# Pairwise bilinear products on one core: VectorE in the order of the text, and a later cut in two loads

## The chip, the cores and the metric

The kernel runs on one core of a Trainium2 chip. The metric is device time in microseconds (us) of one launch: the median of three runs, beside the time of one more execution that was taken with the hardware profiler. Differences below about 0.2% can't be told from no change here.

## The reference

For each of 4096 batch rows there are 32 fields of 64 numbers. Each field is multiplied by a 64x64 matrix W, and every pair of fields i < j (496 pairs) gives an elementwise product of the raw field i and the transformed field j, all in float32:

```python
vid = jnp.einsum('bfd,de->bfe', x, W)
idx_i, idx_j = jnp.triu_indices(F_, k=1)
return x[:, idx_i, :] * vid[:, idx_j, :]
```

The input has 33.6 MB and the output 520 MB, so nearly everything that the core does is to write products to HBM.

## The kernel before

**Tiles.** The batch is cut into 16 tiles of 256 rows. The host lays the data out so that the 128 partitions are two batch halves times 64 numbers, and a "unit" is 128 batch rows of one field (or of one pair): 128 float32, 512 bytes on each partition. A tile of input is 32 units; its output is 496 units.

**Memory.** One buffer, `mem`, of 445 units on each partition holds everything: the input tiles, at the units listed in `XPLACE`, and 70 store slots, listed in `SLOTS` as (number of units, first unit, seams). Slots lie on top of older slots and of input tiles that are no longer needed. The framework adds the waits that follow from overlap: a product that writes a unit waits until an earlier store that reads this unit has landed, and a load waits likewise. `vid`, the transformed fields of one tile, takes all of PSUM.

**Work of a tile.** TensorE makes `vid` from the input tile (line 172). VectorE then runs `tensor_tensor` multiplications (line 196), 345 of them over the 16 tiles. The generator `by_block` gives their order, and `products` cuts each block where a slot ends or where a slot has a seam. A product of m x w pairs has m*w*128 elements on each partition: a 5x16 product shows in the profile as 128x10240. When a product fills a slot up to its end, SP issues one DMA that stores the whole slot (line 199). The output order is the order in which the slots are filled, and a slot may hold the end of one tile and the beginning of the next.

**Loads.** Tile 0 comes first, then tiles 1 to 3 in one DMA, then tiles 5 and 4. Two later groups of five tiles each are loaded behind tile 4 and behind tile 9 (lines 205 to 207 start them, line 151 issues them). `CUTS` splits such a load of 160 fields into three DMAs. `load` returns these as `pieces`, and the next store after them gets a dependency on `pieces[-2]` (lines 200 to 202): SP does not issue it before the last load piece but one has landed. So the fields of the last piece are what may still be under way when SP issues that store. All DMAs, loads and stores, are issued by SP, in the order of the text, on one queue.

```python
CUTS = [[None, [(0, 51), (51, 64)]], [(0, 127), (127, 140), (140, 160)], [(33, 160), (20, 33), (0, 20)]]
...
                store = nc.sync.dma_start(out=out[:, begin:end, :], in_=ot)
                if pieces:
                    behind(store, pieces[-2])
                    pieces.clear()
```

**Order on the engines.** `tc.manual_schedule(engines={SP})` keeps SP's instructions in the order of the text. On the other engines the framework's scheduler orders the instructions; it may put an instruction ahead of an earlier one when it expects that one to wait.

**Slots at the places spoken of below.** Slot 60 is (112, 333): units 333 to 444. Slot 61 is (127, 158). Slot 62 is (127, 285): units 285 to 411. Slot 63 is (127, 64, 94): units 64 to 190. Slots 44, 45 and 46, around the last group of loads, are (120, 176), (116, 297) and (92, 160, 16).

Of the kernel before, what the change touches and what calls it, by code (L numbers as in the profile page):

```python
# [21 lines left out]
    [[6, 7, 8, 9, 10]],  # L22
    [[15, 14, 13, 12, 11]],
]
CUTS = [[None, [(0, 51), (51, 64)]], [(0, 127), (127, 140), (140, 160)], [(33, 160), (20, 33), (0, 20)]]
XPLACE = [317, 349, 381, 413, 32, 0, 285, 317, 349, 381, 413, 128, 96, 64, 32, 0]


# [24 lines left out]
def by_block():  # L53


    def within(lo):
        yield "step", lo, 2, 1, 0
        for k in range(2):
            yield "step", lo, 4, 2, k
        for i in (lo, lo + 8):  # L60
            yield "row", i + 4, i, 4, 4
        yield "row", lo + 8, lo, 8, 8

    yield from within(0)
    yield "row", 16, 0, 16, 16
    yield from within(16)


def products(blocks, at=0):

    for kind, a, b, c, d in blocks:
        if kind == "row":
            rows, n, i0, di, j0, dj = c, d, b, 0, a, 1
        else:
            rows, n, i0, di, j0, dj = 16 // b, c, a, b, a + c + d, b
        r = k = 0
        while r < rows:
            room = BREAKS[bisect_right(BREAKS, at)] - at
            if k or room < n:
                m, w = 1, min(n - k, room)  # L80
            else:
                m, w = min(rows - r, room // n), n
            yield at, m, w, i0 + r * di + k, di, j0 + r * dj, dj
            at += m * w
            if k + w == n:
                r, k = r + m, 0
            else:
                k += w
# [10 lines left out]
@with_exitstack  # L99
def pairwise_bilinear_kernel(  # L100
    ctx: ExitStack,
    tc: tile.TileContext,
    x0: bass.AP,
    x: bass.AP,
    out: bass.AP,
):

    nc = tc.nc
    NT = sum(len(tiles) for group in GROUPS for tiles in group)
    F = x0.shape[1] - 1 - PAD0
    D = P // 2
    NP = F * (F - 1) // 2

    BANK = 512 // C


    ctx.enter_context(tc.manual_schedule(engines={mybir.EngineType.SP}))

    const = ctx.enter_context(tc.tile_pool(name="const", bufs=1))
    psum = ctx.enter_context(
        tc.tile_pool(name="ps", bufs=1, space=bass.MemoryType.PSUM)
    )
    vid = psum.tile([P, F, C], F32)

    mem = const.tile([P, UNITS, C], F32)


    w2 = const.tile([P, D], F32)


    place = XPLACE[0]
    nc.sync.dma_start(  # L136
        out=mem.rearrange("p u c -> p (u c)")[:, place * C - D : (place + F // 2) * C],
        in_=x0.rearrange("p u c -> p (u c)")[:, C - D : (1 + F // 2) * C],
    )
    nc.sync.dma_start(out=mem[:, place + F // 2 : place + F, :], in_=x0[:, 1 + F // 2 : 1 + F, :])  # L140
    nc.vector.tensor_copy(w2, mem[:, place - 1, C - D :])  # L141
    loaded = 1

    def load(tiles, cuts=()):
        nonlocal loaded
        n = len(tiles) * F
        place = XPLACE[tiles[0]]
        at = (loaded - 1) * F
        loaded += len(tiles)
        return [  # L150
            nc.sync.dma_start(out=mem[:, place + lo : place + hi, :], in_=x[:, at + lo : at + hi, :])  # L151
            for lo, hi in cuts or [(0, n)]
        ]

    ready = mybir.DependencyInfo(mybir.DependencyClass.Sync, mybir.DependencyReason.DATA)

    def behind(later, earlier):
        tc.add_manual_dep(later.ins, earlier.ins.name, ready, reason="issued when that has landed")

    pieces = []  # L160
    groups, cuts = iter(GROUPS), iter(CUTS)
    for tiles, parts in zip(next(groups)[1:], next(cuts)):
        pieces = load(tiles, parts)

    for t in range(NT):
        xt = mem[:, XPLACE[t] : XPLACE[t] + F, :]


        for b in range(0, F, BANK):
            for h in range(2):  # L170
                half = slice(h * D, (h + 1) * D)
                nc.tensor.matmul(  # L172
                    vid[half, b : b + BANK, :],
                    lhsT=w2[half, :],
                    rhs=xt[half, b : b + BANK, :],
                    start=True,
                    stop=True,
                )

        for at, m, w, i, di, j, dj in products(by_block(), t * NP):  # L180
            slot = bisect_right(STARTS, at) - 1
            n = m * w
            begin, end = STARTS[slot], STARTS[slot + 1]
            ot = mem[:, SLOTS[slot][1] : SLOTS[slot][1] + SLOTS[slot][0], :]
            o = ot[:, at - begin : at - begin + n, :]
            if m == 1:
                left = xt[:, i : i + w, :]
                right = vid[:, j : j + 1, :].to_broadcast([P, w, C])
            else:
                o = o.rearrange("p (m w) c -> p m w c", m=m)  # L190
                right = vid[:, j : j + (m - 1) * dj + 1 : dj, :].unsqueeze(2).to_broadcast([P, m, w, C])
                if di == 0:
                    left = xt[:, i : i + w, :].unsqueeze(1).to_broadcast([P, m, w, C])
                else:
                    left = xt.rearrange("p (m d) c -> p m d c", d=di)[:, i // di : i // di + m, i % di : i % di + w, :]
            nc.vector.tensor_tensor(o, left, right, ALU.mult)  # L196
            at += n
            if at == end:
# [6 lines that stand above are left out]
        if t + 2 == loaded < NT:  # L205
            (tiles,) = next(groups)
            pieces = load(tiles, next(cuts))
# [45 lines left out]
```

## Time and profile before

| what | value |
|---|---|
| median of 3 runs (lowest, highest) | 1291.11 us (1290.9, 1291.38) |
| the profiled execution | 1290.48 us |
| its span, first to last instruction | 1288.7 us |
| TensorE clock granted, mean | 0.55 |
| HBM read, written | 33.59 MB, 520.09 MB |
| TensorE matmuls | 219.6 us in 512 instructions |
| VectorE idle until a store had landed | 168.1 us in 37 waits |

The profiled execution is 0.63 us below the median, and 1.8 us of it lie outside the span. "Landed" is the moment at which a DMA's semaphore is complete; the list of DMA issues gives the time from issue to landing. In the slices of the page each digit is a share in tenths, and 9 means 90% or more. When a window of a few microseconds is cut into slices, a packet (a piece of up to 65 KB, about 2.4 us on one DMA engine) counts in the slice in which it starts, so single slices there are spiky, and only a long run of zeros means idle engines. The trace also records every DMA packet with its start, duration and size; where the text gives times of single packets, they come from there. On each of the 16 DMA engines the last packet of a DMA is a write of 4 bytes, and from these one sees when each engine was through with that DMA.

### The profile page before, as it was taken

Reading aid. Unit: us, or ns where it says so; the run is one execution under the profiler, and the core shown is the slowest. Engines: PE = TensorE matmul, PEld = TensorE weight load, DVE = VectorE, ACT = ScalarE, POOL = GpSimd, SP = SyncE. Lnnn points to the kernel's source line nnn. Section 1 sums busy time; section 2 is a strip of 40 time slices with the busy share of each in tenths; the row PEclk is TensorE's granted clock in tenths of the full one; section 3 lists DMA queues with packets and bytes.
Section 4 is the critical chain, followed back from the end, with each engine's and each line's share of the span. In section 5 each row is a group of like instructions: output and inputs, shape, how many; then the busy total and the mean of one; then the engine's idle time right before and its main releaser. Section 6 shows DMA issues by size and latency. Waiting matters only on the chain.

```text
span 1288.7 us, 1651 instructions
## 1 busy us (share of the span) xinstructions
PE 219.6 (17%) x512; PEld 42.2 (3%) x512; DVE 1084.0 (84%) x346; POOL 0.2 (0%) x4
## 2 busy tenths in 40 slices
PE   4031221203120213040312111103031130312000
PEld 1000000000000000000000000000000000000000
DVE  6899988899967389899799992859999889999942
POOL 0000000000000000000000000000000000000000
PEclk8555555656555556565555655555555565555555
DMA  9999999999999999999999999999999999989999
GB/s 416 432 423 439 443 436 423 434 424 443 420 453 411 422 435 431 443 439 430 423 442 427 433 443 430 423 418 432 447 433 418 441 440 418 448 361 452 435 414 412
DMA packets 11672, 553.78 MB, mean 430 GB/s; under 512 B 1296, under 2 KB 1296, under 8 KB 1680
## 3 DMA queue, kind: packets, MB, share of 16 engines
q1 hardware_dynamic: 11664, 553.69, 99.6%
q8 instruction: 4, 0.07, 0.0%
q14 instruction: 4, 0.03, 0.0%
HBM read 33.59 MB, written 520.09 MB: 430 GB/s over the span
## 4 chain that ended last, share of the span: by engine, by line
DMA 50%; DVE 42%; issue 6%; DVEq 0%; SPq 0%
DMA out_dram<-mem 45%; DVE mem L196 42%; DMA mem<-in_r_x_dram 5%; DVEq L241 0%; SPq L151 0%; DVEq L196 0%; SPq L140 0%; SPq L136 0%; SPq L199 0%
## 5 line engine op out<-in xcount | busy, mean ns | idle before, releaser
L196 DVE TENSOR_TENSOR mem<-mem,vid 128x1024 f32<-128x1024 f32 (+16 forms) x345 | 1083.8, 3213 | 173.6 <-DMA out_dram<-mem 168.1
L172 PE MATMUL vid<-mem,w 64*64 64x512 f32 x512 | 219.6, 988 | 961.1 <-DVE mem L196 853.3
L172 PEld LDWEIGHTS vid<-mem,w 64*64 64x64 f32 x512 | 42.2, 198 | 1137.3 <-DVE mem L196 984.8
L141 DVE COPY w<-mem 128x64 f32<-128x64 f32 x1 | 0.2, 195 | 5.8 <-DMA mem<-in_r_x_dram 5.8
L221 POOL MEMSET const-bfloat16-1.0<- 128x1 bf16 x1 | 0.1, 102 | 0.0
L221 POOL MEMSET const-uint8-127<- 128x1 uint8 x1 | 0.1, 102 | 0.0
L221 POOL MEMSET const-float32-0.0<- 128x1 f32 x1 | 0.1, 98 | 0.2 <-issue 0.2
L221 POOL MEMSET const-float32-1.0<- 128x1 f32 x1 | 0.1, 98 | 0.0
## 6 DMA issues: line engine op xcount, KB each, us to landing
out_dram<-mem SPq DMA_DIRECT2D x15, 8128.0 KB, 28.3
out_dram<-mem SPq DMA_DIRECT2D x14, 7680.0 KB, 24.6
out_dram<-mem SPq DMA_DIRECT2D x6, 7168.0 KB, 26.2
out_dram<-mem SPq DMA_DIRECT2D x5, 7936.0 KB, 28.1
out_dram<-mem SPq DMA_DIRECT2D x3, 7424.0 KB, 22.6
out_dram<-mem SPq DMA_DIRECT2D x3, 5888.0 KB, 20.9
mem<-in_r_x_dram SPq DMA_DIRECT2D x2, 8128.0 KB, 38.7
out_dram<-mem SPq DMA_DIRECT2D x2, 8064.0 KB, 24.4
```

The lines of the kernel that those rows point to most:

```text
L141: nc.vector.tensor_copy(w2, mem[:, place - 1, C - D :])
L172: nc.tensor.matmul(vid[half, b : b + BANK, :], lhsT=w2[half, :], rhs=xt[half, b : b + BANK, :], start=True, stop=True,)
L196: nc.vector.tensor_tensor(o, left, right, ALU.mult)
L221: nc = _bacc.Bacc("TRN2", target_bir_lowering=False, num_devices=1, dynamic_dma_scratch_size=1024)
```

## The change

```diff
-CUTS = [[None, [(0, 51), (51, 64)]], [(0, 127), (127, 140), (140, 160)], [(33, 160), (20, 33), (0, 20)]]
+CUTS = [[None, [(0, 51), (51, 64)]], [(0, 127), (127, 134), (134, 160)], [(33, 160), (26, 33), (0, 26)]]
...
-    ctx.enter_context(tc.manual_schedule(engines={mybir.EngineType.SP}))
+    ctx.enter_context(tc.manual_schedule(engines={mybir.EngineType.SP, mybir.EngineType.DVE}))
```

The first edit moves the boundary between the second and the third piece of the two large loads: the second piece shrinks from 13 fields to 7, and the third grows from 20 to 26. The store behind each of the two loads, which waits for the second piece, is thus issued with 26 fields left under way in place of 20. The loads' total size and the number of DMAs stay. The second edit keeps VectorE's instructions, too, in the order of the text. TensorE's order remains the scheduler's.

## The prediction

> **What bounds the kernel now.** I read the page first, for the engine that is never free:
>
> ```profile
> span 1288.7 us, 1651 instructions
> ...
> PE 219.6 (17%) x512; PEld 42.2 (3%) x512; DVE 1084.0 (84%) x346; POOL 0.2 (0%) x4
> ...
> DMA  9999999999999999999999999999999999989999
> GB/s 416 432 423 439 443 436 423 434 424 443 420 453 411 422 435 431 443 439 430 423 442 427 433 443 430 423 418 432 447 433 418 441 440 418 448 361 452 435 414 412
> ...
> q1 hardware_dynamic: 11664, 553.69, 99.6%
> ```
>
> The 16 DMA engines are busy throughout; VectorE, at 84%, has room. One slice stands out: the 36th (1127.6 to 1159.8 us) has an 8 and 361 GB/s. So the time is bytes over DMA rate plus the time in which DMA engines have nothing to do, and such time lies in one place. I asked for the DMA view of 1125 to 1145 us, in slices of 0.5 us:
>
> ```profile
> DMA  9029980299502000000009000090000900009000
> GB/s 520 0 130 910 650 390 0 130 1300 390 260 0 130 0 0 0 0 0 0 0 0 2081 0 0 0 0 2081 0 0 0 0 2081 0 0 0 0 2081 0 0 0
> ```
>
> From 1131.5 to 1135.5 us no packet but one starts. By the packet records the engines end the store before at 1131.68 (first) to 1133.56 (last) and all start the next at about 1135.81; idle time, averaged over the 16, is 3.74 us. Elsewhere after the first load it sums to under 0.6 us. The chain of waits for 1090 to 1160 us says who was late:
>
> ```profile
> 1096.97 11.13 DVE mem L196 x6
> 1108.10 0.99 issue
> 1109.09 25.89 DVE mem L196 x8
> 1134.98 20.59 DMA out_dram<-mem
> ```
>
> VectorE works without a break until SP issues a store at 1134.98. The issues around it (DMA view of windows at 1089.3 and at 1106.7) show when the two stores before it land:
>
> ```profile
> out_dram<-mem SPq DMA_DIRECT2D x1, 7168.0 KB, 25.9
> ...
> out_dram<-mem SPq DMA_DIRECT2D x1, 8128.0 KB, 27.3
> ```
>
> The first is slot 60 (1089.29 + 25.9 = 1115.2), the second slot 61 (1106.74 + 27.3 = 1134.0). So slot 62 was issued 0.95 us after the queue's last store had landed. Why was VectorE late? The groups of 1111.0 to 1141.6 us, shapes apart:
>
> ```profile
> L196 DVE TENSOR_TENSOR mem<-mem,vid 128x10240 f32<-128x10240 f32 x1 | 10.8, 10809 | 0.0
> L196 DVE TENSOR_TENSOR mem<-mem,vid 128x7168 f32<-128x7168 f32 x1 | 7.6, 7611 | 0.0
> L196 DVE TENSOR_TENSOR mem<-mem,vid 128x2048 f32<-128x2048 f32 x3 | 6.8, 2276 | 0.0
> ...
> L196 DVE TENSOR_TENSOR mem<-mem,vid 128x768 f32<-128x768 f32 x1 | 0.9, 943 | 0.0
> ```
>
> Slot 62 wants, after its 33rd unit, two 4x4 products (2048 elements; the third in the group is another slot's), one 7x8 (7168) and one 1x6 (768). The 5x16 product (10240) belongs to slot 63 and stands after them in the text. In the trace it runs first, from 1111.36 to 1122.09, inside the last products of slot 62. I compared the shapes of all 345 products with the order that the generator gives: only here and at one place near 798 us does the trace differ from the text.
>
> **What the Trainium skill says.** "DMA: Bandwidth & Descriptors", section "Queues, rings and completion order": each DMA engine consumes its queue in ring order. The trace agrees; each engine starts a DMA right behind its own part of the one before. The section "Why a DMA increments its semaphore by 16 and not by 1" of that page: the engines finish independently and only the full count means landed. Here the 16 ends are 1.88 us apart before the gap and 0.16 us apart after it (1155.06 to 1155.22). The section "Specifications": the fabric's ceiling is 435 GB/s. In steady stretches stores land at 434 to 435 GB/s, so nothing is to be won from the rate.
>
> **Edit 1, VectorE in the order of the text, near 1111 us.** The scheduler had a reason: the first 4x4 product writes units 318 to 333, and unit 333 is read by slot 60's store, which lands at 1115.17. In the order of the text VectorE therefore idles from 1111.36 to 1115.22, 3.86 us. Then, by the starts in the trace (a product starts some 0.08 us before its forerunner's end): 2.20 + 2.20 + 7.53 + 0.94 = 12.87 us, and slot 62 is full at 1128.09. SP issues it at 1128.1, 6.9 us earlier. First packets come 0.83 us after an issue (1134.98 to 1135.81), so at 1128.95, before the first engine is free at 1131.68. The gap is gone.
>
> What it is worth: the end is set by the DMA engine that is last. It ended at 1133.56 and finished slot 62's store at 1155.22, after 21.66 us. Such a store (65024 bytes per partition) takes the last engine 19.17 us while the engines are apart (landings at 1061.22 and 1080.39): 2.49 us saved. The seven stores after it landed 19.24, 19.27, 18.76, 18.15, 19.24, 18.74 and 18.88 us apart with the engines in step; with the engines apart, as before the gap, stores of these sizes took 19.17, 19.17, 18.69, 18.10, 19.17, 18.69, and scaled 18.83: 132.28 - 131.82 = 0.46 us more. Sum 2.95 us. Bounds: 2.27 us, the last engine's own idle time (1133.56 to 1135.83), if it doesn't catch up; 3.74 us, the mean idle time of all 16, if it catches up fully. I take 2.95.
>
> What is late next: VectorE's idle 3.86 us reappears at slot 63, whose 5x16 product now comes last: full at 1145.4 instead of 1141.5. The store before lands at 1134.04 - 0.12 + 19.17 = 1153.1 (slot 61's landing trailed its last packet by 0.48 us, 0.12 more than others), 7.7 us later. Slot 64 is full at 1162.8 against a landing at 1172.3. VectorE's own waits of 1.46, 0.20, 1.41 and 1.53 us, all for landings that now come 2.5 to 2.9 us earlier, take up the delay; the last wait (15.03 us at 1250.32) moves with the landings. The smallest margin remains slot 69's 5.5 us. So the 3.86 us cost nothing.
>
> **Edit 1, near 798 us.** A 512-element product (0.68 us) of slot 46 ran ahead at 798.59, in VectorE's wait for a landing (to 809.40). In the text's order it follows at 835.3, in another such wait (17.64 us, to 852.99). Nothing.
>
> **Edit 2, the cut.** 6 fields are 393 KB, 0.9 us at 434 GB/s: SP issues the held stores at about 427.9 and 830.9 instead of 428.78 and 831.74. Before, the first engine was through with the loads at 429.60 and 832.58 and began the store at 429.62 and 832.61: at most 0.03 us is to be had, on engines that are not the last. Load packets cost bytes/27.03 plus 7 ns, with the count unchanged: nothing. The following stores on SP queue behind the held one, but they were ready within 2 us and had 17 us to spare. A loss can't be excluded by the trace of before: at the opposite turn, from store to load (402 and 805 us), the last store packets took 2384 in place of 2291 ns, and store plus load landed 1.24 us late. With loads then stores the last engine had its store's descriptors ready 1.8 us ahead and lost nothing (14.54 and 18.14 us, full rate). I take 0; the range holds 0 to 1.24 us at each of two places.
>
> Sum against the profiled execution: 1290.48 - 2.95 = 1287.5. Its time is 0.63 us under the median, so the median becomes 1291.11 - 2.95 = 1288.2.
>
> **Rivals.**
> - The turn costs: one or both held stores disturb the loads' tail by 1.24 us, 1289.4 to 1290.6. For: the opposite turn. Against: the last engine's case above. 10%.
> - No gain, 1291.1: the gap reopens elsewhere, or the scheduler's semaphores hold slot 62 back. It needs slot 62 to be full 5 us later than worked out. For: in-order VectorE can no longer pass over a late landing. Against: margins of 5 us or more at all other stores. 13%.
> - Slower: TensorE, which stays with the scheduler, is ordered anew around the fixed VectorE, and a group of matmuls that VectorE needs comes after those of the whole tile. A tile's matmuls are 219.6/16 = 13.7 us; a store has about 5 us of margin, so VectorE's wait counts from 5 us on, and one such tile costs 13.7 - 5 = 8.7 us net of its margin: 1297. Against: VectorE waited for TensorE once, 5.4 us, at the start. 10%.
> - More than worked out, 1287.0: a refill of instructions that now falls on another engine than the last one. 5%.
>
> **How the numbers follow.** 62% for 1288.2 (own range 1287.4 to 1288.9). What a measurement can tell from no change is 0.2%, 2.6 us: faster means below 1288.5. Of the main case about four fifths lie there: 0.62 x 0.8 + 0.04 = 0.54. Slower 0.10, the rest 0.36. The range of 1287.2 to 1291.2 takes in the first two rivals and leaves out the slow one and the tail.
>
> **What would show it.** Right: the 10240-element product after the 768 one; an idle VectorE of about 3.9 us before 1115.2; slot 62 issued near 1128; no empty slices at 1131 to 1136; slot 63 near 1145; the 16 ends of the last store 1 to 2 us apart; held stores issued 0.9 us earlier with no change in landings. Wrong: landings after 427 or 831 us that come later by a microsecond; a new store issued after the landing of the one before; VectorE waits on TensorE after the first tile.

## The result and the profile after

| | before | after |
|---|---|---|
| median of 8 runs (lowest, highest) | 1290.95 us (1290.4, 1291.38) | 1287.17 us (1286.98, 1287.57) |
| ratio, 95% interval | | 0.9971 (0.9962 to 0.9981) |
| the profiled execution, its span | 1290.48 us, 1288.7 us | 1287.35 us, 1285.6 us |

The change makes the kernel 3.8 us faster. That is 0.8 us more than forecast, and 1287.17 us lies 0.03 us below the low end of the stated range. The range was counted from a before of 1291.11 us; before measured 0.16 us less in this series.

The page of the kernel after, the lines that answer to those of before:

```profile
span 1285.6 us, 1654 instructions
...
PE 220.4 (17%) x512; PEld 42.4 (3%) x512; DVE 1083.6 (84%) x346; POOL 0.2 (0%) x4
...
DMA  9999999999999999999999999999999999999998
GB/s 414 419 440 440 436 420 447 420 442 418 443 432 431 428 433 420 438 438 429 445 423 447 434 419 439 419 426 435 438 433 422 441 439 423 443 427 427 434 443 385
...
q1 hardware_dynamic: 11664, 553.69, 99.8%
```

The 36th slice has a 9 and 427 GB/s now; only the last slice, in which the last store runs out, is below. The DMA view of 1125 to 1145 us, again in slices of 0.5 us:

```profile
DMA  5059565095659990699505985059555098256980
GB/s 260 0 260 1300 260 260 260 0 1300 260 260 260 390 910 520 0 260 780 780 260 0 260 1170 390 260 0 260 1300 260 260 260 0 1300 390 130 260 260 1170 390 0
```

The long run of zeros is gone: no two slices in a row are empty. VectorE, in the timeline of 1105 to 1150 us (start, length, what, and in brackets the idle time before it):

```profile
1114.69 41.39 DVE L196 TENSOR_TENSOR mem<-mem,vid 128x2048 f32<-128x2048 f32 x12 [2.61 <-DMA out_dram<-mem]
```

and in the groups of 1111 to 1117 us, shapes apart:

```profile
L196 DVE TENSOR_TENSOR mem<-mem,vid 128x2048 f32<-128x2048 f32 x2 | 4.5, 2282 | 2.6 <-DMA out_dram<-mem 2.6
```

So VectorE now waits 2.61 us for slot 60's landing, then runs slot 62's two 2048-element products; the 10240-element product is no longer ahead of them. SP issues slot 62 at 1127.60 us in place of 1134.98. Its issue line (DMA view at 1127.6 us) shows the landing, 1127.60 + 25.3 = 1152.9 us:

```profile
out_dram<-mem SPq DMA_DIRECT2D x1, 8128.0 KB, 25.3
```

The store ahead of it lands at 1133.74 us, so slot 62 is in the queue 6.1 us early.

### The profile page after: what moved, and what is told of

It reads as the page before. It is cut to its first block, busy times and chain, and to the rows that moved or that the text cites. A ratio compares the mean times of both kernels' runs of the same rounds, so it can differ in the third digit from the quotient of the medians.

```text
span 1285.6 us, 1654 instructions
## 1 busy us (share of the span) xinstructions
PE 220.4 (17%) x512; PEld 42.4 (3%) x512; DVE 1083.6 (84%) x346; POOL 0.2 (0%) x4
## 4 chain that ended last, share of the span: by engine, by line
DMA 46%; DVE 46%; issue 6%; DVEq 0%; SPq 0%
DVE mem L196 46%; DMA out_dram<-mem 41%; DMA mem<-in_r_x_dram 5%; DVEq L241 0%; SPq L151 0%; DVEq L196 0%; SPq L140 0%; SPq L136 0%; SPq L199 0%
## 5 line engine op out<-in xcount | busy, mean ns | idle before, releaser
L196 DVE TENSOR_TENSOR mem<-mem,vid 128x1024 f32<-128x1024 f32 (+17 forms) x345 | 1083.4, 3213 | 170.8 <-DMA out_dram<-mem 165.1
```

## The experiments

Each kernel is timed beside the kernel before on the same chip. The experiments are four series, each on another chip, and the median of before in them is 1291.03 to 1291.19 us, so a few tenths of a microsecond between kernels of different series are weak evidence. Traces are of one execution each. "Fields left" is the size of the last piece of a large load. All but the one with the cut alone have VectorE in the order of the text.

### Which edit, and which product

**Order alone.** The kernel before with the second edit only:

```diff
-    ctx.enter_context(tc.manual_schedule(engines={mybir.EngineType.SP}))
+    ctx.enter_context(tc.manual_schedule(engines={mybir.EngineType.SP, mybir.EngineType.DVE}))
```

> VectorE in the order of the text, the cut left at 140 and 20. Theory (the order fills the gap near 1131 us, the cut gives nothing): the whole gain, 1287.2 us, ratio 0.997; no empty slices at 1131 to 1136 us, slot 62 issued near 1127 us. If the cut costs about 0.6 us at the loads, as the shift of the landings after 427 and 831 us in the changed kernel suggests, this one is up to 0.6 us faster than the changed kernel: 1286.6 us. Rival (the cut is what helps): 1291 us.

Measured: 1288.12 us (1287.77 to 1288.56), ratio 0.9976 (0.9968 to 0.9985): 2.91 us faster than before. Slot 62 is issued at 1129.06 us. The DMA view of 1125 to 1145 us:

```profile
DMA  9920299202962029903098029920299202952029
GB/s 910 910 130 0 130 1431 390 130 0 130 1561 260 130 0 130 1561 390 0 130 0 1561 390 0 130 520 1300 130 0 130 1300 520 130 0 130 1561 260 130 0 130 1561
```

No gap. The order explains 2.9 of the 3.8 us. The suspicion that the cut costs something, read from one pair of traces, fell: without the cut the kernel is 0.95 us slower than the changed one, and the ranges of the runs don't touch.

**Cut alone.** The kernel before with the new `CUTS` line only.

> The cut at 134 and 26 alone, VectorE left to the scheduler. Theory: no gain, 1291.0 us, the gap near 1131 us stays; if the cut costs at the loads, landings after 427 and 831 us come 0.4 to 0.7 us later than before, and part of it vanishes in the gap, where all engines start together: at most 1291.5 us. Rival (the cut is what helps): 1287.2 us.

Measured: 1291.09 us (1290.8 to 1291.49), ratio 1.0002 (0.9993 to 1.001). The DMA view of 1125 to 1145 us:

```profile
DMA  5229552992623000000000090000900009000090
GB/s 260 130 130 1300 260 260 130 520 1040 130 260 130 130 0 0 0 0 0 0 0 0 0 0 2081 0 0 0 0 2081 0 0 0 0 2081 0 0 0 0 2081 0
```

The gap is there, and the cut gives nothing. So the cut is worth 0.95 us with the gap filled and nothing with it.

**One product back.** The changed kernel, with slot 63's 5x16 product put ahead of slot 62's last four and slot 63's first product, as the scheduler had it. The place near 798 us stays in the order of the text.

```diff
-        for at, m, w, i, di, j, dj in products(by_block(), t * NP):
+        listed = list(products(by_block(), t * NP))
+        if t == 14:
+            k = [p[0] for p in listed].index(7064)
+            listed.insert(k - 5, listed.pop(k))
+        for at, m, w, i, di, j, dj in listed:
```

> The changed kernel with one product moved: the 5x16 product of slot 63 stands ahead of the two 4x4 products of slot 62 again, as the scheduler had it; the other reordering, near 798 us, stays undone. Theory (this one product makes the gap): the whole gain is gone, 1291 us, slot 62 issued near 1135 us. Rival (the place near 798 us, or fixed order as such, gives the gain): 1287.2 us.

Measured: 1291.11 us (1290.89 to 1291.56), ratio 1.0001 (0.9992 to 1.0009). The chain of waits of this kernel for 1090 to 1165 us:

```profile
1108.61 0.99 issue
1109.60 25.89 DVE mem L200 x8
1135.49 20.59 DMA out_dram<-mem
1156.08 0.02 issue
```

The store is issued at 1135.49 us again, and the chain has the shape that it had before. One product out of 345 makes the gap, and the other reordering is worth nothing that shows.

### Why the cut is worth 0.95 us

**No hold.** The changed kernel without the hold behind the two large loads (the first one, behind tiles 5 and 4, stays):

```diff
                 if pieces:
-                    behind(store, pieces[-2])
+                    if t < 4:
+                        behind(store, pieces[-2])
                     pieces.clear()
```

> The changed kernel without the hold behind the two large loads: the two stores are issued as soon as their slots are full. Theory (the held stores' time of issue is covered by the loads in flight, so its size doesn't matter once descriptors are there in time): 1287.2 us within 0.5. Rival (a store that is ready behind a load disturbs the load's tail, more the earlier it is ready): 1288 to 1290 us, with the landings of the loads' pieces after 427 and 831 us later by half a microsecond or more.

Measured: 1288.26 us (1287.9 to 1288.51), ratio 0.9978 (0.997 to 0.9986): 1.1 us slower than the changed kernel, and the last pieces of the loads land 0.5 and 0.4 us later. The rival holds. SP's timeline of 815 to 833 us shows the second store issued 13 us earlier than in the changed kernel (831.51):

```profile
818.71 0.34 SPq L199 DMA_DIRECT2D out_dram<-mem  x1
```

In the packet records, packets of the last load piece (13312 bytes, about 0.50 us each) that took over 0.15 us more than most packets of this size, and the time that slow packets add, in the mean of the 16 engines:

```
                 first load     second load    time added, first and second load
changed kernel   3 of 128       0 of 128       0.03 us, under 0.01 us
without hold     31 of 128      31 of 128      0.74 us, 0.86 us
```

So stores that are ready far ahead do disturb the end of a load, and this is what the hold is good for. Single slow packets occur with the hold, too: a second trace of the changed kernel has three, one of them 1.15 us longer than the others.

**21, 28 and 32 fields left.** The changed kernel with other boundaries in both loads: (127, 139) and (21, 33), then (127, 132) and (28, 33), then (127, 128) and (32, 33). Theory B arose because TensorE, with the new cut, has one more instruction that only waits (12 in place of 11), and because its fourth refill of instructions moved from 1113 to 1102 us; the page counts the four refills in this line:

```profile
q8 instruction: 4, 0.07, 0.0%
```

> The changed kernel with 21 fields left in place of 26 (pieces end at 139, and begin at 21). A boundary inside a group of four fields gives TensorE one more wait, as with 26 and unlike with 20, and so its fourth refill of instructions falls near 1102 us as in the changed kernel, not near 1113. Theory A (the 0.95 us between 20 and 26 fields comes from the time of issue: with 20 the DMA engines that are through first wait for the held store): 1287.9 us, a little better than with 20, first store packets later than the first engine's end by up to half a microsecond. Theory B (it comes from the moved refill): 1287.2 us.

> The changed kernel with 28 fields left. The boundary falls between groups of four, so TensorE has as many waits as with 20, and the refill falls near 1113 us. Theory A (time of issue): 1287.2 us or a little less, no idle engines at the turn. Theory B (the moved refill): 1288.1 us.

> The changed kernel with 32 fields left, the store issued 0.9 us earlier still. If a store that is ready ahead of the loads' end disturbs their tail, as the slow load packets of the kernel without the hold suggest, it shows here first: some load packets of the last piece 0.2 to 0.8 us longer, and 1287.3 to 1288 us, between 26 fields and no hold (1288.26 us). If the disturbance needs a store that is ready long before: 1287.2 us.

Measured: 21 fields 1287.56 us (1287.34 to 1288.48), between the theories. 28 fields 1287.26 us (1286.93 to 1287.53), but TensorE has the one more instruction there, too, and the refill fell at 1101 us, so that run didn't tell the theories apart. 32 fields 1287.74 us (1287.21 to 1288.06): half a microsecond lost, as the first case of its expectation had it. Only one and three packets of the last pieces were slow, 0.07 us in the mean of an engine at each load, but that trace is of the fastest execution of this kernel; what the half microsecond went to is not shown. From 20 over 26 to 32 fields and to no hold, the time falls and rises again; 26 and 28 can't be told apart.

**The refill moved, the cut not.** Order alone, plus two matmuls of tile 0 issued twice (the last group of fields, both halves), which shifts TensorE's refills.

```diff
+            if t == 0 and b == F - BANK:
+                nc.tensor.matmul(vid[half, b : b + BANK, :], lhsT=w2[half, :], rhs=xt[half, b : b + BANK, :], start=True, stop=True)
```

> VectorE in the order of the text, the cut at 140 and 20 as before, and two of tile 0's matmuls issued twice (the last group of fields, both halves), so that TensorE's stream is some instructions longer and its fourth refill falls near 1100 us in place of 1114. Theory A (the 0.95 us between 20 and 26 fields is the time of issue): 1288.1 us, as with the order alone. Theory B (the moved refill): 1287.2 us.

Measured: 1287.81 us (1287.62 to 1288.55), with the refill at 1100.6 us: 0.31 us under the order alone, 0.6 above the changed kernel. So the moved refill alone doesn't bring the 0.95 us; whether it brings a third of them can't be told, since the two ranges overlap. The third refill moved as well, from 833.2 us with the order alone to 765.9.

**One load at a time.** The new cut in the second load only, then in the first only, and the changed kernel once more as the measure.

```diff
-[(0, 127), (127, 134), (134, 160)], [(33, 160), (26, 33), (0, 26)]
+[(0, 127), (127, 140), (140, 160)], [(33, 160), (26, 33), (0, 26)]    second load only
+[(0, 127), (127, 134), (134, 160)], [(33, 160), (20, 33), (0, 20)]    first load only
```

> VectorE in the order of the text, and the new cut at the second large load alone (26 fields left there, 20 at the first). The boundary inside a group of four fields, which gives TensorE its one more wait, is that of the first large load, so here the refill falls near 1114 us as before. Theory A (time of issue, mostly at the second load, where engines were seen idle with 20 fields left): 1287.4 us. Theory B (the moved refill): 1288.1 us.

> VectorE in the order of the text, and the new cut at the first large load alone (26 fields left there, 20 at the second); TensorE has its one more wait and the refill falls near 1101 us. Theory A: 1287.9 us. Theory B: 1287.2 us.

> The changed kernel itself, beside the two, as the measure for them: 1287.2 us.

Measured: second only 1287.48 us (1287.34 to 1287.75) with the refill at 1114.9 us; first only 1287.81 us (1287.47 to 1288.29) with the refill at 1100.5; changed kernel 1287.22 us (1287.0 to 1287.34). Theory A had 1287.4 and 1287.9, theory B 1288.1 and 1287.2. As the whole account B falls. First only and the changed kernel ran in one series, have the third and the fourth refill at the same places within a microsecond (832.4 and 1100.5, 832.2 and 1101.5 us), and differ in the cut at the second load alone: it gives 0.59 us. The other 0.3 us can't be given to the first load: where its cut is made, the fourth refill moves with it, and the kernel with the refill moved and no new cut has the same 1287.81 us as first only. Second only differs from the order alone in its third refill, too (768.3 us). Each against its own before, the gains are 2.91 us for the order alone, 3.38 with the refill moved, 3.37 first only, 3.70 second only and 3.96 for the changed kernel.

The packet records show the wait that A is about. From the profiled executions, with the time at which the first DMA engine is through with the load and the time of the held store's first packet:

```
                 fields left   first load             second load
                               first through, store   first through, store
before           20, 20        429.60, 429.62         832.58, 832.61
order alone      20, 20        429.67, 429.95         832.88, 833.51
refill moved     20, 20        429.68, 429.83         832.82, 832.82
first load only  26, 20        429.83, 429.83         831.96, 832.71
second only      20, 26        429.85, 429.85         832.85, 832.85
changed kernel   26, 26        429.83, 429.83         832.29, 832.39
changed, again   26, 26        429.69, 429.69         831.84, 831.84
```

With 20 fields left the engines that are through first wait up to 0.75 us for the store; with 26 they wait 0.10 us at most. SP's timeline for "order alone" and for "first load only" has these issues, each just after the landing of the second piece (832.60 and 831.81 us):

```profile
832.67 0.34 SPq L199 DMA_DIRECT2D out_dram<-mem  x1
```

```profile
831.87 0.34 SPq L199 DMA_DIRECT2D out_dram<-mem  x1
```

When this happens can be worked out. Landing, issue and first packet follow the end of the second piece on the engine that is last by 1.3 us (831.32 to 832.61 before). The last piece of 20 fields takes an engine 8 packets of 385 ns, 3.1 us. So the first engines run dry when the 16 are more than 3.1 - 1.3 = 1.8 us apart. They were 2.39 us apart with the order alone and 2.54 with the first load only; before and with the refill moved, 1.80 and 1.77. With 26 fields the last piece takes 4.0 us and the bound is 2.7 us.

The wait is only a part of the 0.95 us. In the mean of the 16 engines, the delay of the one that ran the third refill left out, it was 0.40 us for both loads of order alone (whose trace is of its slowest execution, 1288.56 us) and 0.40 us at the second load of first only, against 0.59 us that the cut there is worth. With the refill moved it was 0.05 us for both loads, in an execution at the median of that kernel, which is still 0.6 us slower than the changed one.

**A hold at the other turn.** The changed kernel with the store ahead of each large load cut in two, and the load held until the larger part has landed:

```diff
-                store = nc.sync.dma_start(out=out[:, begin:end, :], in_=ot)
+                split = end - LEFT if slot in (21, 43) else end
+                store = nc.sync.dma_start(out=out[:, begin:split, :], in_=ot[:, : split - begin, :])
+                if split < end:
+                    ahead = store
+                    nc.sync.dma_start(out=out[:, split:end, :], in_=ot[:, split - begin :, :])
...
             pieces = load(tiles, next(cuts))
+            behind(pieces[0], ahead)
```

> The changed kernel with the same kind of hold at the other turn: the store ahead of each of the two large loads is cut in two DMAs, its last 26 units apart, and the load's first piece is issued only when the larger part has landed, some 4 us before the store is through in place of 18. Theory (descriptors of the other direction, ready long ahead, disturb the packets in flight): the last store packets take 2.3 us again, not 2.8 to 3.4, the first load packets 2.4, and the two turns give back 0.5 to 1.2 us each on the engine that is last: 1285 to 1286.2 us. Rival (the turn from stores to loads costs this by itself): 1287.2 us, or a little more for the added DMAs.

Measured: 1287.48 us (1287.04 to 1287.83), ratio 0.9972 (0.9962 to 0.9983). The theory falls. The loads were issued at 402.69 and 805.34 us, but packets on both sides of the turn were as slow as before: in the changed kernel the excess of those over 0.2 us sums to about 14.8 and 14.3 us over the 16 engines around the two loads, and here to 13.7 and 17.2 us. It moved from the last store packets to the first load packets. The turn from stores to loads costs each engine about 0.9 us (14.5/16), whether the load is issued 18 us or 3.5 us before the store is through.

## Why the prediction was right, and where its size was off

- **What bounds the kernel, and the gap.** Right. The time is set by the DMA engines, and one product's place made their only gap: putting that product back alone took the whole gain away.
- **Edit 1 near 1111 us.** Right in each step. Forecast: VectorE idle for 3.86 us until 1115.2, slot 62 issued at 1128.1, slot 63 full at 1145.4. The changed kernel: idle for 2.61 us until 1114.69, issued at 1127.60, slot 63 issued at 1144.91. The order alone saved 2.91 us where the sum had 2.95, so the forecast of 1288.2 us fits that kernel.
- **The sum by the last engine.** Right in kind: the 16 ends of the last store are 1.41 us apart in the changed kernel, against 0.16 before, and the landings after slot 62 are 19.16, 19.13, 18.69, 18.10, 19.17, 18.70 and 18.86 us apart, within 0.04 us of those used. But the 0.46 us that the sum takes from these landings is not a slower rate: in the mean over the engines the seven stores took 132.28 us in the trace of before and 132.14 in the changed kernel. The rest of it is the last engine gaining on the others, whose distance shrinks from 1.72 to 1.41 us.
- **What is late next.** Right: no store was issued after the landing of its forerunner, and slot 69's margin is 5.49 us.
- **Edit 1 near 798 us.** Right: nothing, shown together with the product put back.
- **Edit 2, the cut.** This is the term that was mis-sized: taken as 0, with a loss as the only thing that could come, it measured a gain of 0.9 us once the gap was filled. The step that failed was "at most 0.03 us is to be had, on engines that are not the last". The 0.03 us was read from one execution in which the engines happened to be 1.8 us apart, just at the bound; with the order alone they were 2.39 us apart and waited 0.63 us. And engines that are not the last do count. In the traces of order alone, refill moved, first only, 21 fields and the changed kernel, the engine that ends last is none of those that were last at the loads: it is the one on which the fourth refill ran. It was 0.1 to 0.4 us ahead of the mean of the 16 before the refill and 1.3 to 1.5 us behind the mean after it (in the changed kernel the next engine ends only 0.05 us earlier). With the gap, all engines start anew at a time that VectorE sets, so a lead is thrown away; this is in keeping with the cut alone giving nothing (slot 62 issued at 1135.98 us there, 1134.98 before). The part of the 0.9 us that is not waiting remains open, as said below.
- **The opposite turn.** The 2384 ns that the prediction gives for the last store packets ahead of a load is the mean of all 128 packets of that store. The last packet of each engine took 2.29 to 3.36 us, 3.0 in the mean.
- **Signs named ahead.** Issue of the held stores 0.9 us earlier: 0.5 and 0.2 us in the first trace of the changed kernel, 1.1 and 1.0 in the second, so one trace doesn't measure this. "No change in landings": wrong. The last pieces landed 0.72 and 0.63 us later than before in the first trace, 1.05 and 0.47 in the second; a microsecond was named as a sign of being wrong. The kernel was faster all the same. A landing tells of the last engine, and 15 others were ahead.
- **The rivals.** The disturbed tail of a load is real, but it needs a store that is ready for longer than with 26 fields; it shows without the hold. The slow case didn't come: VectorE waited for TensorE once, 5.5 us, at the start. The rival of a moved refill had 1287.0 us, close to what was measured, but for another reason: in the first trace of the changed kernel its engine is still the last, and the cut at the second load gains with the refills in place. A part of the 0.9 us may be the refill's all the same; no run here settles it.

What stays open: which part of the 0.3 us is the first load's and which the refill's, and where the gain lies beyond the wait. Something of it is seen in the stores between the loads. The 21 stores between the two loads took 364.1 to 364.3 us in the mean over the engines in all five kernels with 20 or 21 fields at the first load in which this was worked out (before, order alone, refill moved, 21 fields, second load only), and 363.3 to 363.5 us in the five with 26 to 32 (changed kernel twice, first load only, 28, 32). When the first store behind the load is through, the last engine is 2.38 us and more behind the first in the second set, and under 1.9 us in the first. So these stores take some 0.8 us less in the mean where the engines are further apart. But without the hold and with the load held they took 362.8 and 363.0 us at 2.33 and 2.01 us, so the distance alone doesn't set their time. No run here varied it alone, and a gain in the mean need not reach the engine that ends last.

## What to carry to other kernels

In a kernel whose DMA engines are busy all the time, look for the one slice in which they are not, and ask which product the late store waited for: an order that fills a wait on VectorE can cost more in the store queue than it saves. A hold that lets stores follow a load has two sides: with too much left under way the loads' end is disturbed, with too little the engines that are through first wait. What is left should take an engine longer than the distance between the first and the last DMA engine plus the time to the first packet of the store (here 1.8 to 2.7 us plus 1.3). Test such a cut only after larger gaps are closed, since a gap hides what it is worth.

## What was not expected of the hardware

- A store that is ready in the queue behind a load slows the load's last packets: 0.74 and 0.86 us in the mean of an engine, with 31 of 128 packets slow. A load behind a store costs about 0.9 us per engine at the turn, and holding the load back didn't change it.
- Landings come closer together when the DMA engines are apart: a store of 65024 bytes per partition lands 19.24 to 19.27 us after the one before it with the ends 0.16 us apart (before), and 19.13 to 19.18 us after it with the ends 1.4 to 1.8 us apart (order alone, changed kernel). Most of this is the last engine gaining on the others. The mean over the engines differs by 0.08 and 0.14 us over seven stores.
- A refill of 16 KB of TensorE's instructions runs as one packet on one DMA engine (0.88 to 0.96 us) and slows the packets beside it by 0.3 to 0.6 us, so its engine falls 1.3 to 1.9 us behind. In the mean this hardly shows, but it can decide which engine ends last. The two stores spanning the fourth refill took 36.19 to 36.29 us in the mean over the engines wherever it fell (1100 to 1115 us).
